# A selective scan laid out by states: sixteen states of eight channels in a tile's rows

## The chip, the cores and the metric

The kernel runs on one core of one Trainium2 chip. The metric is the device time of one execution in microseconds; three executions took 6134.04, 6134.65 and 6145.41 us, median 6134.65.

The core's engines work side by side, each through its own list of instructions in order: PE (matrix products; PEld is its loading of weights), DVE (element-wise work, reductions, the scan instruction), ACT (functions with scale and bias), POOL (element-wise work too) and SP, which here only issues transfers (DMA). They meet at semaphores.

## The reference, cut to what matters

The input is 4 images of 128 channels and 64 x 64 pixels, that is 4 x 4096 positions. Layer 0 normalizes, does a 3 x 3 depthwise convolution with a small network behind it, and then a selective scan ("Mamba"); layer 1 is attention with 4 heads over the 4096 positions of an image, and then a mixture of 8 experts of which each position takes 2. The change is in the scan. The 128 channels are cut into 4 chunks of 32, and each chunk is a sequence of its own that is widened to 64 channels `d` with 16 states `n` each:

```python
x_dbl = xin @ x_proj_w.T
dt, Bm, Cm = jnp.split(x_dbl, [R, R + N], axis=-1)
delta = jax.nn.softplus(dt @ dt_proj_w.T + dt_proj_b)
A = -jnp.exp(A_log)
dA = jnp.exp(delta[..., None] * A)                          # position, d, n
dBu = delta[..., None] * Bm[:, :, None, :] * xin[..., None]

def step(h, inp):
    dA_t, dBu_t, C_t = inp
    h = dA_t * h + dBu_t
    y = jnp.einsum('bdn,bn->bd', h, C_t)
    return (h, y)
...
y = jnp.transpose(ys, (1, 0, 2)) + D_skip * xin
out = y * jax.nn.silu(z) @ out_proj_w.T
```

So `delta` and `xin` depend on the channel and not on the state, `B` and `C` on the state and not on the channel, and `A` on both. All is float32.

## The kernel before, in words

**Units of the scan.** An image's 4096 positions are cut into 8 blocks of 512 (`BLK`). A block's 4 chunks are taken in two halves `p` of two chunks: 2 x 64 channels are the 128 rows of a tile. The scan of one block and half is 16 units, one for each state `n`; four images, eight blocks, two halves and 16 states make 1024 units (line 1110). A unit is:

- `fetched` (line 724): one transfer spreads the rows B and C of state n, which lie in DRAM as `bcd`, over the 128 rows (tile `rows`, 4 buffers, 512 KB),
- `decayed` (734): ACT makes `da` = exp(delta x A_n); A_n is a column of `amat`, one number a row,
- `scan` (739): DVE makes `h` = B x `du` (`du` is delta x xin), runs the scan instruction over the 512 positions in place, with the last column of the block before as its start (`states`), and makes `hc` = C x `h`.

The 16 `hc` of a half are to be added up into `y`. PE does this by products with the identity that accumulate in a PSUM tile (`ps_y`). In image 0 each `hc` goes through PE; in images 1 to 3 POOL first adds each odd `hc` to the even one before it, and PE takes the sum (lines 1153 to 1160). Then `scanned` (752) adds the skip term and gates.

**Where a unit's operands come from.** `inputs(b, i, p)` (675) makes `xin`, the gate `zs`, B and C (`bc`, written out to `bcd`), and on ACT and POOL `delta` by way of `e`, `ln` and `lost`, and `du`; these two stay in SBUF. `first_norm` (570) and `conv` (605) stand before it, `closed` (761) after the scan of a block: it projects, normalizes, and writes the attention's operands to DRAM.

**The order.** Nothing is planned at run time. The function runs one Python loop (line 1113) over slots and records each engine's instructions in the order in which they are called; the helper in line 445 adds a dependency from each instruction to the one before on its engine, so all instructions carry that line, and groups in the profile are told apart by their tiles. In each slot the loop

1. issues the transfers that earlier stages left (`flush`, 464), and the `rows` of the unit three slots ahead; if that unit's `inputs` are not done yet, `until` (1074) pushes the lanes on until they are,
2. lets one group of attention for an image whose scan is over run its scores: four products `sc` and two exponentials `pT` on ACT; its products with the values, `av` (two 64-column halves side by side), come at the end of the following slot (`weighted`, 910),
3. does the sum products that are due (1130): one slot after the unit in image 0, two slots after the odd unit in images 1 to 3; a PE instruction behind them waits with them,
4. has ACT save the state of the unit before (a copy of the last column, not in an image's last block) and make `da` of the next unit, and DVE do the three instructions of this unit,
5. between these, moves two lanes of generators on by half a stage each: lane Y (`group_norm`, `first_norm`, `conv`, `inputs`) and lane X (`closed`, the division and output stages of attention, the experts). Each lane has one PSUM tile, `ps_X` or `ps_Y`.

So image 0's scan has no attention beside it, images 1 to 3 have that of the image before, and the last image's attention runs alone. All transfers of the loop are in SP's list, in the order of the calls. Lane Y's temporaries rotate through four buffers (`tmp`, 488).

Of the kernel before, what the change touches and what calls it, by code (L numbers as in the profile page):

```python
# [9 lines left out]
F32 = mybir.dt.float32  # L10
# [7 lines left out]
P = 128  # L18
C = 128
EPS = 1e-5  # L20
BLK = 512
NT = BLK // P
IMG = 64
DI = 64
# [12 lines left out]
def conv_mamba_attn_moe_kernel(ctx: ExitStack, tc: tile.TileContext, t: dict):  # L37
# [35 lines left out]
    inz, cb, dtb, dsk, wbc = (load(k) for k in ("inz", "cb", "dtb", "dsk", "wbc"))  # L73
# [21 lines left out]
    amat = const.tile([P, NST], F32, name="amat")  # L95
# [579 lines left out]
    def inputs(b, i, p):  # L675

        xn, pairs = xn_of[b, i], pairs_of[b, i]
        r = slice(DI * p, DI * p + DI)
        ps = work("Y")
        summed(ps, [(inxc[:, j, :], pairs[:, p, 2 * j : 2 * j + BLK]) for j in range(2)])  # L680
        pz = work("X")
        mm(pz, inz[r, :], xn[r, 3 : 3 + BLK])
        yield
        xin = mix.tile([P, BLK], F32, name="xin", bufs=2)
        scalar.activation(xin, ps, AF.Silu, bias=cb)
        zs = mix.tile([P, BLK], F32, name="zs", bufs=4)
        scalar.activation(zs, pz, AF.Silu)
        yield

        pb = work("X")  # L690
        mm(pb[0:DI, :], wbc, xin)
        ps = work("Y")
        mm(ps, wdt, xin)
        yield
        bc = mix.tile([DI, BLK], F32, name="bc")
        scalar.copy(bc, pb[0:DI, :])
        bcd = dram.tile([2, NST, 2 * BLK], F32, name="bcd", bufs=4)
        send(bcd.rearrange("c n (k q) -> (c n k) q", k=2), bc)

        e = mix.tile([P, BLK], F32, name="e")  # L700
        scalar.activation(e, ps, AF.Abs, bias=dtb)
        scalar.activation(e, e, AF.Exp, scale=-1.0)
        ln = mix.tile([P, BLK], F32, name="ln")
        scalar.activation(ln, e, AF.Ln, bias=1.0)
        delta = mix.tile([P, BLK], F32, name="delta", bufs=2)
        scalar.activation(delta, ps, AF.Relu, bias=dtb)
        yield
        yield

        lost = mix.tile([P, BLK], F32, name="lost")  # L710
        gpsimd.tensor_scalar(lost, e, 1.0, -1.0, ALU.add, ALU.add)
        gpsimd.tensor_sub(lost, e, lost)
        gpsimd.tensor_add(ln, ln, lost)
        gpsimd.tensor_add(delta, delta, ln)
        du = mix.tile([P, BLK], F32, name="du", bufs=2)
        gpsimd.tensor_mul(du, delta, xin)
        in_of[b, i, p] = xin, zs, delta, du, bcd
        yield
        yield
        yield  # L720
# [3 lines left out]
    def fetched(b, i, p, n):  # L724

        bcd = in_of[b, i, p][4]
        w = mix.tile([P, 2, BLK], F32, name="rows", bufs=4)
        sync.dma_start(
            out=w.rearrange("p k q -> p (k q)"),
            in_=bcd[:, n, :][None].to_broadcast([DI, 2, 2 * BLK]),  # L730
        )
        return w

    def decayed(b, i, p, n):
        da = mix.tile([P, BLK], F32, name="da", bufs=3)
        scalar.activation(da, in_of[b, i, p][2], AF.Exp, scale=amat[:, n : n + 1])
        return da

    def scan(b, i, p, n, w, da):

        du = in_of[b, i, p][3]
        h = mix.tile([P, BLK], F32, name="h", bufs=3)
        vector.tensor_mul(h, w[:, 0, :], du)
        vector.tensor_tensor_scan(
            out=h, data0=da, data1=h, initial=0.0 if i == 0 else states[b % 2][:, p, n : n + 1],
            op0=ALU.mult, op1=ALU.add,
        )
        hc = mix.tile([P, BLK], F32, name="hc", bufs=5)
        vector.tensor_mul(hc, w[:, 1, :], h)
        return h, hc  # L750

    def scanned(b, i, p, y):
        xin, zs, delta, du, bcd = in_of.pop((b, i, p))
        vector.scalar_tensor_tensor(xin, xin, dsk, y, ALU.mult, ALU.add)
        gpsimd.tensor_mul(zs, xin, zs)
        gated[b, i, p] = zs
# [355 lines left out]
    even, y_of, waiting, groups, image, slot = None, {}, None, None, 0, 0  # L1112
    while slot < len(units) or due or waiting or groups or image < B or lanes["X"] or running:
# [16 lines left out]
        while due and due[0][0] <= slot:  # L1130
            _, unit, term, first = due.popleft()
            b, i, p, n = unit
            if first:
                y_of[b, i, p] = ps_y.tile([P, BLK], F32, name="y")
            mm(y_of[b, i, p], ident, term, first, n == NST - 1)
            if n == NST - 1:
# [9 lines left out]
        for ahead in range(slot if slot == 0 else slot + 1, min(slot + 2, len(units))):  # L1146
            decays[ahead] = decayed(*units[ahead])
        if slot < len(units):
            unit = units[slot]
            h, hc = scan(*unit, rows.pop(slot), decays.pop(slot))  # L1150
            old = unit, h
            b, i, p, n = unit

            if b == 0:
                due.append((slot + 1, unit, hc, n == 0))
            elif n % 2 == 0:
                even = hc
            else:
                gpsimd.tensor_add(even, even, hc)
                due.append((slot + 2, unit, even, n == 1))  # L1160
# [34 lines left out]
def _laid_out(i):  # L1195
# [11 lines left out]

    def twice(a):
        return np.repeat(a, 2, axis=0)
# [4 lines left out]
    wbc = np.zeros((P, 2, NST, 2), np.float32)  # L1214
    xdt, dtT = np.zeros((4, P), np.float32), np.zeros((4, P), np.float32)
    for c in range(2):
        d = slice(c, P, 2)
# [14 lines left out]
    for h in range(NH):  # L1232
# [19 lines left out]
        "wbc": wbc.reshape(P, -1), "alog": twice(c0["A_log"]),  # L1252
# [28 lines left out]
```

## Time and profile before

| | |
|---|---|
| median of 3 executions | 6134.65 us |
| the profiled execution | 6135.26 us; span from first to last instruction 6133.5 us |
| PE busy | 5188.5 us (85%) |
| DVE busy | 4197.3 us (68%) |
| ACT busy | 3952.4 us (64%) |
| POOL busy | 1925.1 us (31%) |
| granted PE clock, mean | 0.921 |
| transfers | 928.55 MB, 44.7% of the time of 16 engines on SP's queue |
| `pT` on ACT | 2048 x 1024 ns |
| scan on DVE, with a state | 896 x 1451 ns |
| `hc` and `h` on DVE | 1024 x 782 ns and 1024 x 777 ns |
| `hc`+`hc` on POOL | 384 x 1451 ns |
| sum products on PE | 640, two passes each, 804.2 us busy |
| `rows` from DRAM | 1024 x 512 KB, 4.2 us from issue to landing |

Times are in microseconds from the first instruction unless marked ns. A group's line gives line, engine, operation, output and inputs by tile names, the operand shapes and count, then busy time and mean duration, then the idle time of the engine just before these instructions and what ended it. The row of slices gives, for 40 equal parts of the span, an engine's busy share in tenths, and the clock that PE was granted in tenths of full speed. The chain of waits goes back from the last instruction to what released it, step by step; its shares say which work set the end. Matrix products are pipelined and their ends modelled, so that the distance between their starts is the better measure of what one costs.

### The profile page before, as it was taken

Reading aid. Unit: us, or ns where it says so; the run is one execution under the profiler, and the core shown is the slowest. Engines: PE = TensorE matmul, PEld = TensorE weight load, DVE = VectorE, ACT = ScalarE, POOL = GpSimd, SP = SyncE. Lnnn points to the kernel's source line nnn. Section 1 sums busy time; section 2 is a strip of 40 time slices with the busy share of each in tenths; the row PEclk is TensorE's granted clock in tenths of the full one; section 3 lists DMA queues with packets and bytes.
Section 4 is the critical chain, followed back from the end, with each engine's and each line's share of the span. In section 5 each row is a group of like instructions: output and inputs, shape, how many; then the busy total and the mean of one; then the engine's idle time right before and its main releaser. Section 6 shows DMA issues by size and latency. Waiting matters only on the chain.

```text
span 6133.5 us, 60705 instructions
## 1 busy us (share of the span) xinstructions
PE 5188.5 (85%) x18378; PEld 2135.6 (35%) x18378; DVE 4197.3 (68%) x7155; ACT 3952.4 (64%) x6052; POOL 1925.1 (31%) x1757
## 2 busy tenths in 40 slices
PE   4666665698899989889999898999888898999996
PEld 2222222233333333333333333333333333333332
DVE  4888887788888877778888777888777772021112
ACT  3445544577777767677777676777777765655652
POOL 2334323444344334333444344344333320000000
PEclk7777777799999999999999999999999999999996
DMA  3444554555455535555555554555554542212210
GB/s 99 163 174 164 187 178 152 171 190 170 168 184 178 188 134 181 167 170 179 187 178 181 178 168 168 177 167 174 174 167 165 170 158 79 79 64 72 74 66 13
DMA packets 359137, 928.55 MB, mean 151 GB/s; under 512 B 37633, under 2 KB 120978, under 8 KB 358802
## 3 DMA queue, kind: packets, MB, share of 16 engines
q1 hardware_dynamic: 357634, 923.80, 44.7%
q8 instruction: 148, 2.42, 0.2%
q14 instruction: 187, 1.53, 0.1%
q10 hardware_dynamic: 1168, 0.80, 0.0%
HBM read 806.95 MB, written 100.66 MB: 148 GB/s over the span
## 4 chain that ended last, share of the span: by engine, by line
PE 43%; DVE 33%; ACT 12%; POOL 5%; issue 5%; DMA 2%; SPq 0%; DVEq 0%; ACTq 0%; POOLq 0%
PE av L445 18%; DVE h L445 15%; PE ps_X L445 10%; PE sc L445 9%; DVE hc L445 5%; DVE acc L445 5%; PE y L445 4%; ACT pT L445 3%; PE ps_Y L445 3%; DVE cm L445 3%; ACT L445 2%; ACT xt L445 2%; POOL rsX L445 2%; POOL rsY L445 1%; ACT da L445 1%
## 5 line engine op out<-in xcount | busy, mean ns | idle before, releaser
L445 ACT ACTIVATE pT<-sc 128x1024 f32<-128x1024 f32 x2048 | 1986.7, 1024 | 881.2 <-PE sc L445 876.3
L445 PE MATMUL av<-pT,v 128*64 128x512 f32 x8192 | 2027.1, 616 | 0.0
L445 DVE TENSOR_TENSOR_SCAN h<-da,state,h 128x512 f32<-128x512 f32 x896 | 1299.8, 1451 | 244.0 <-ACT da L445 157.8
L445 PE MATMUL sc<-qs,ks 128*128 128x512 f32 x4096 | 1335.2, 444 | 124.5 <-ACT pT L445 77.4
L445 POOL TENSOR_TENSOR hc<-hc 128x512 f32<-128x512 f32 x384 | 557.1, 1451 | 1707.3 <-DVE hc L445 1542.9
L445 PEld LDWEIGHTS sc<-qs,ks 128*128 128x128 f32 x4096 | 714.3, 192 | 726.5 <-ACT pT L445 367.8
L445 PE MATMUL y<-hc,ident 128*128 128x512 f32 x1280 | 804.2, 718 | 181.7 <-DVE hc L445 172.5
L445 PEld LDWEIGHTS av<-pT,v 128*64 128x64 f32 x8192 | 506.9, 139 | 1168.0 <-issue 1140.3
L445 DVE TENSOR_TENSOR hc<-rows,h 128x512 f32<-128x512 f32 x1024 | 801.2, 782 | 70.9 <-DVE h L445 1.4
L445 DVE TENSOR_TENSOR h<-rows,du 128x512 f32<-128x512 f32 x1024 | 795.9, 777 | 32.3 <-POOL du L445 29.2
L445 ACT ACTIVATE da<-delta,amat 128x512 f32<-128x512 f32 x1024 | 750.2, 734 | 25.8 <-DVE h L445 24.3
L445 DVE SCALAR_TENSOR_TENSOR acc<-ps_X,pr,acc 128x128 f32<-128x128 f32 x1024 | 358.4, 350 | 304.6 <-PE ps_X L445 276.8
L445 ACT ACT_TABLE_LOAD x318 | 408.0, 1283 | 101.8 <-PE sc L445 92.1
L445 POOL TENSOR_SCALAR rsX<-mvX 128x4 f32<-128x4 f32 x97 | 52.4, 540 | 1224.3 <-DVE mvX L445 1222.7
L445 PE MATMUL ps_X<-w_ew,xf 128*128 128x512 f32 x512 | 304.3, 678 | 126.0 <-DVE acc L445 123.9
L445 PEld LDWEIGHTS y<-hc,ident 128*128 128x128 f32 x1280 | 260.3, 222 | 419.8 <-DVE hc L445 302.8
L445 DVE RECIPROCAL rden<-ps_X 128x8 f32<-128x8 f32 x64 | 13.1, 205 | 566.9 <-PE ps_X L445 566.9
L445 ACT COPY state<-h 128x1 f32<-128x1 f32 x896 | 176.3, 197 | 269.6 <-DVE h L445 269.2
L445 ACT ACTIVATE xt<-ps_Y,shiftY,rsY 128x128 f32<-128x128 f32 x380 | 142.9, 460 | 174.3 <-POOL shiftY L445 158.2
L445 DVE TENSOR_TENSOR_SCAN h<-da,h 128x512 f32<-128x512 f32 x128 | 176.9, 1382 | 57.0 <-ACT da L445 45.8
L445 POOL TENSOR_SCALAR rsY<-mvY 128x4 f32<-128x4 f32 x95 | 43.5, 458 | 532.7 <-DVE mvY L445 528.0
L445 PE MATMUL ps_Y<-ident,xt 128*128 128x128 f32 x380 | 74.7, 329 | 159.8 <-ACT xt L445 159.5
(197 smaller groups left out, 4766.6 us busy)
## 6 DMA issues: line engine op xcount, KB each, us to landing
rows<-bcd SPq DMA_DIRECT2D x1024, 512.0 KB, 4.2
ks<-kd SPq DMA_DIRECT2D x256, 512.0 KB, 5.6
v<-vd SPq DMA_DIRECT2D x256, 256.0 KB, 5.9
qs<-qd SPq DMA_DIRECT2D x64, 512.0 KB, 5.8
pairs<-xn SPq DMA_DIRECT2D x128, 128.5 KB, 2.4
qd<-hi SPq DMA_DIRECT2D x32, 512.0 KB, 6.8
qd<-lo SPq DMA_DIRECT2D x32, 512.0 KB, 5.9
vd<-vst SPq DMA_DIRECT2D x32, 512.0 KB, 7.4
```

What stands on the lines that cost most here:

```text
L445: return lambda *args, **kw: queued(op(*args, **kw))
```

## The change

Rows of a unit are now 16 states of 8 channels (row = 8 x state + channel), in place of 128 channels of one state. A block's half still has 16 units `k`, each with 8 of the 128 rows of (chunk, channel).

- B and C of a chunk, spread over the 8 channels of each state, are fetched once for 8 units (tile `bcs`, 2 buffers, 512 KB) and stay.
- `delta` and `du` are made in one tile `dd`, written to DRAM (`ddd`, 512 KB), and for each unit 8 of their rows are fetched, spread over the 16 states (`rows`, 512 KB as before). `inputs` has two more half stages for it. `da` is made from the fetched `rows`, not from the resident `delta`; `amat` has 8 columns, one for each group of 8 channels.
- `y` of a unit is a sum over its 16 states, so over rows. Four units' `hc` are kept and summed together, one slot after the fourth: for each a product with 128 x 32 weights `sel` that puts its 8 channels at 8 of 32 output rows; the four go to the four 32-row strips of the `y` tile, side by side. Sixteen products a half fill the tile, in four groups. POOL adds nothing.
- Weights, biases and `A` are laid out so that the channels stand in the order this gives (`place`).
- Buffers: `da` 3 to 2, `hc` 5 to 6, `e` and `ln` move to lane Y's four temporaries, `lost` to the place of `du`.

```diff
-        e = mix.tile([P, BLK], F32, name="e")
+        dd = mix.tile([P, 2, BLK], F32, name="dd")
+        delta, du = dd[:, 0, :], dd[:, 1, :]
+        e = tmp("Y", "e")
...
-        in_of[b, i, p] = xin, zs, delta, du, bcd
+        yield
+        yield
+        ddd = dram.tile([P, 2 * BLK], F32, name="ddd", bufs=4)
+        send(ddd, dd.rearrange("p k q -> p (k q)"))
+        in_of[b, i, p] = xin, zs, ddd, bcd
...
+    def fetched(b, i, p, k):
+        ddd, bcd = in_of[b, i, p][2:]
+        if k % 8 == 0:
+            w = mix.tile([P, 2, BLK], F32, name="bcs", bufs=2)
+            sync.dma_start(
+                out=w.rearrange("p k q -> p (k q)"),
+                in_=bcd[k // 8][:, None, :].to_broadcast([NST, P // NST, 2 * BLK]),
+            )
+            chunk[0] = w
         w = mix.tile([P, 2, BLK], F32, name="rows", bufs=4)
+        at = 32 * (k % 4) + 8 * (k // 4)
         sync.dma_start(
             out=w.rearrange("p k q -> p (k q)"),
-            in_=bcd[:, n, :][None].to_broadcast([DI, 2, 2 * BLK]),
+            in_=ddd[at : at + 8][None].to_broadcast([NST, P // NST, 2 * BLK]),
         )
-        return w
+        return w, chunk[0]
...
-        da = mix.tile([P, BLK], F32, name="da", bufs=3)
-        scalar.activation(da, in_of[b, i, p][2], AF.Exp, scale=amat[:, n : n + 1])
+        da = mix.tile([P, BLK], F32, name="da", bufs=2)
+        scalar.activation(da, w[:, 0, :], AF.Exp, scale=amat[:, k % 8 : k % 8 + 1])
...
-        vector.tensor_mul(h, w[:, 0, :], du)
+        vector.tensor_mul(h, bc[:, 0, :], w[:, 1, :])
...
-        hc = mix.tile([P, BLK], F32, name="hc", bufs=5)
-        vector.tensor_mul(hc, w[:, 1, :], h)
+        hc = mix.tile([P, BLK], F32, name="hc", bufs=6)
+        vector.tensor_mul(hc, bc[:, 1, :], h)
...
-            mm(y_of[b, i, p], ident, term, first, n == NST - 1)
-            if n == NST - 1:
+            for g, term in enumerate(four):
+                mm(y_of[b, i, p][32 * g : 32 * g + 32, :], sel[:, q, :], term, q == 0, q == 3)
+            if q == 3:
...
-            if b == 0:
-                due.append((slot + 1, unit, hc, n == 0))
-            elif n % 2 == 0:
-                even = hc
-            else:
-                gpsimd.tensor_add(even, even, hc)
-                due.append((slot + 2, unit, even, n == 1))
+            terms.append(hc)
+            if len(terms) == 4:
+                due.append((slot + 1, unit, terms))
+                terms = []
...
+    for q in range(4):
+        sel[:, :, q, q] = np.eye(8)
```

## The prediction

> **What bounds the kernel now.** First the forty slices, then the same engines by stage. The scan's units start at 101 us; image 0's end at 1078 and the last at 5026, so stage I is scan alone, stage II scan of images 1 to 3 beside attention of the image before, stage III attention alone.
>
> ```profile
> PE   4666665698899989889999898999888898999996
> DVE  4888887788888877778888777888777772021112
> PEclk7777777799999999999999999999999999999996
> ...
> 101.00:1078.00 977.00, 623.24 (x1256) 240.37 (x1257) 821.86 (x1167) 472.09 (x904) 330.44 (x296) 0.76 0.49 169
> 1078.00:5026.00 3948.00, 3513.68 (x13045) 1465.21 (x13043) 3147.66 (x5130) 2872.85 (x4441) 1549.04 (x1360) 0.96 0.52 174
> 5026.00:6133.00 1107.00, 1010.10 (x3966) 411.05 (x3964) 205.16 (x740) 584.23 (x670) 25.51 (x52) 0.95 0.19 63
> ```
>
> The stage rows give PE, PEld, DVE, ACT, POOL busy, PE clock, DMA share and GB/s. Stage I is DVE's (84%; PE 64% at a clock of 0.76). Stage II has PE at 89% and DVE at 80%; stage III is PE's. Busy shares don't say what a saved microsecond is worth, so next the chain of waits, by stage (II, then I), and a piece of II:
>
> ```profile
> by line: PE av L445 15.4%; DVE h L445 15.1%; PE ps_X L445 8.5%; PE sc L445 7.5%; DVE hc L445 5.2%; issue 5.1%; DVE acc L445 5.0%; ACT pT L445 4.7%; PE y L445 4.6%; DVE cm L445 3.7%; PE ps_Y L445 2.9%; ACT L445 2.7%; ACT xt L445 1.9%; POOL r
> ...
> by line: DVE h L445 34.0%; DVE hc L445 12.8%; PE y L445 6.7%; PE ps_X L445 5.7%; issue 4.6%; PE ps_Y L445 4.1%; ACT L445 3.9%; POOL rsY L445 3.2%; DMA rows<-bcd 2.8%; ACT xt L445 2.7%; ACT da L445 2.0%; POOL rsX L445 1.9%; DVE cm L445 1.7%;
> ...
> 3042.37 0.93 PE sc L445 x4
> 3043.30 0.86 PE y L445 x2
> 3044.16 1.87 PE av L445 x8
> ```
>
> One sum product (two passes, as each of these float32 products is) costs 0.86 us of chain; `av`, eight passes on 64 columns, costs 1.87, that is 0.47 for every two passes: those go two abreast, as their starts show:
>
> ```profile
> 3000.11 0.65 PE L445 MATMUL av<-pT,v 128*64 128x512 f32 x2
> 3000.59 0.60 PE L445 MATMUL av<-pT,v 128*64 128x512 f32 x2
> 3001.02 0.60 PE L445 MATMUL av<-pT,v 128*64 128x512 f32 x2
> ```
>
> Last the scan's own groups, stage II above stage I:
>
> ```profile
> L445 DVE TENSOR_TENSOR_SCAN h<-da,state,h 128x512 f32<-128x512 f32 x672 | 998.7, 1486 | 176.1 <-ACT da L445 111.9 <-DVE h L445 2.3 <-ACT xt L445 0.5
> L445 DVE TENSOR_TENSOR h<-rows,du 128x512 f32<-128x512 f32 x768 | 608.0, 792 | 0.0
> L445 DVE TENSOR_TENSOR hc<-rows,h 128x512 f32<-128x512 f32 x768 | 591.1, 770 | 55.9 <-DVE h L445 0.9
> L445 POOL TENSOR_TENSOR hc<-hc 128x512 f32<-128x512 f32 x383 | 555.8, 1451 | 1700.1 <-DVE hc L445 1542.9 <-PE sc L445 99.7 <-PE av L445 14.5
> L445 DVE TENSOR_TENSOR_SCAN h<-da,h 128x512 f32<-128x512 f32 x96 | 136.1, 1417 | 45.5 <-ACT da L445 36.9
> ...
> L445 DVE TENSOR_TENSOR_SCAN h<-da,state,h 128x512 f32<-128x512 f32 x224 | 301.1, 1344 | 67.9 <-ACT da L445 45.9 <-DVE h L445 0.9
> L445 DVE TENSOR_TENSOR hc<-rows,h 128x512 f32<-128x512 f32 x256 | 210.0, 820 | 14.9 <-DVE h L445 0.5
> L445 DVE TENSOR_TENSOR h<-rows,du 128x512 f32<-128x512 f32 x256 | 187.9, 734 | 32.3 <-POOL du L445 29.2 <-DMA rows<-bcd 3.0
> L445 DVE TENSOR_TENSOR_SCAN h<-da,h 128x512 f32<-128x512 f32 x32 | 40.8, 1276 | 11.5 <-ACT da L445 8.8
> ```
>
> **The change, part by part** (stage II unless said; 192 groups of four units there, 64 in stage I).
>
> 1. *Sums on PE.* 383 products cost 383 x 0.86 = 330 us. Four 32-column products abreast would cost 0.86 a group, 165 in all. Added: changes of column width. `xin`x`wbc`, 64 columns between 128-column products, takes 1.04 to 1.07 where 0.86 would do, so 0.09 a change, one or two a group: about 26. Net -139. Only 4.6% x 3948 = 182 of the 330 us stand on the chain (55%), so the gain lies between 55% (-76) and all of it, PE being 89% busy; I take three quarters: **-104**. No row shows four abreast: with two it is 330 again, one by one 660.
> [...]
>
> 2. *POOL's 383 adds go.* DVE's two multiplies and scan take 2333.9/768 = 3.04 us a unit in II and 739.8/256 = 2.89 in I, where no such adds run: 0.15 x 768 = 114 us. Their weight on the chain: `h` 15.1% x 3948 = 596 of 1743 busy (34%), `hc` alike. **-40**; ends 0 (POOL's other work stretches DVE instead) and -114.
> [...]
>
> 3. *A tighter wait.* A pair's product now waits for POOL, PE only 8 us for it in all; a group's waits for the `hc` of the slot before, one unit later, in PE's fixed order, with that slot's `av` and the lanes' products behind it. I set each start of a product against the end of that `hc`: 80 of 383 would be late, by 102 us; half the products remain: 51, and in some 40 cases the fourth product then runs alone, 0.86 each: 85 in all, 55% of it on the chain: **+45**; ends 0 and +100, as a faster PE waits more.
>
> 4. *Stage I.* The sums fall from 256 x 0.86 to 64 x 0.86; 6.7% x 977 = 65 us of them are on the chain, three quarters go: -49. But PE, idler, may lose clock: `ps_X` and `ps_Y` hold 9.8% = 96 us at 0.76; at 0.5 they cost 48 more. DVE's work stays. **-10**; ends -50 and +50.
>
> 5. *Fewer slots.* The sum of a half block is due a slot earlier, so `closed` of the last image starts at slot 1029, not 1034, and the loop written out has 1329 slots, not 1334. Stage III has 1107/310 = 3.57 us a slot, -18; four attention groups move into II (2.8 us of PE each). **-7**; ends -18 and 0.
>
> 6. *The way through DRAM.* Before the first unit the pair delta, du is now written out (512 KB; `qd<-hi`, as large, lands after 6.8 us) and fetched (4.2): **+11** at the start; ends +6 and +17. `inputs` has two more stages, so the first half block's inputs end just at the slot that fetches them (61, 93, ...). Elsewhere `du` ends 16 us before that unit's `da` starts, against 0.5 issue + 6.8 + 4.2 + 2.5 for the B/C tile fetched ahead of it = 14: hidden by the units still running; in stage I 10.4 us, and `h` 6 later. At the last block of images 0 to 2, where the loop already stops to push the lane (19.7, 31.8, 30.6 us between two units' starts against 3 to 5), 8 pushes take the place of 6, 7 and 7; at some 4 us each 16, part of it lane work done sooner, and in image 0 `du` ends 5.5 us before `h`, so some 8.5 late: **+22**; ends +9 and +40.
>
> At nothing: 512 KB a unit is fetched as before, and 192 more transfers of 512 KB (100 MB on 928) take the DMA share from 0.52 to about 0.57; cover gone, rows come late. `da` now waits for its rows: in II it starts 8.6 us or more after their issue in 99 of 100, against 4.2 (longest 9.8), and rows are freed a scan and a multiply earlier. On SP the new write waits for `du`, and rows, `ks`, `v` wait behind it; they are issued three slots (15 us) ahead. `da` with two buffers: ACT's state copy, just before it, waits for that same scan already. `e` and `ln` in the lane's four buffers, host layouts, the 64 KB `sel`: beside the start's other loads.
>
> Sum: -104 - 40 + 45 - 10 - 7 + 11 + 22 = -83. The profiled execution took 6135.3 (span 6133.5), the median is 6134.65, so they agree: 6135 - 83 = **6052**, say 6050.
>
> **Rivals.** *Two abreast only:* `av` proves two, nothing proves four. Term 1 becomes +20 for width changes, stage I gains half: 6052 + 124 + 5 = 6180, slower; it decides once a group takes over about 1.45 us. One by one: 330 x 0.75 more still, 6430. *The DRAM way shows:* if write plus fetch exceed 16 us, DVE waits at each of 28 half-block borders; 5 us each is +140, 6190. Against it: 14 by medians; for it: both run amid 170 GB/s. *Fuller relief:* PE's saving counts whole (-139), DVE's 114, no new wait, stage I -50: 5860 to 5920; for it speaks that the two engines that lead stage II's chain are relieved at once, against it the 80 late products. *Nothing moves* (the chain merely changes engine, as ACT's 73% could let it): 6120 to 6147.
>
> **How the numbers follow.** What this kernel's runs can tell from no change is about 0.2%, 12 us. Main case 0.60 (own range 5960 to 6115), two abreast 0.13, one by one 0.03, DRAM 0.10, fuller relief 0.14. Faster: 0.14 and nearly all of the main case, less 0.01 from elsewhere, 0.69; same 0.04; slower 0.27. The range 5900 to 6190 leaves out one by one and about half of DRAM and of fuller relief: some 0.16.
>
> **What would show it.** Right: `y` passes starting in fours some 10 ns apart, two rounds a group, its busy time in II near 200 us; no `hc<-hc`; scan near 1340 ns in II; PE waiting for `hc` by tens of us, not hundreds; stage II near 3870. Wrong: `y` in four or more rounds, ACT `da` waiting for `rows`, SP long on `du`, DVE idle at each border, or a clock in stage I far under 0.7 with DVE waiting for `ps_Y`.

## The result: slower by 2.3%, and the profile after

The changed kernel takes 6282.7 us, the median of 4 executions (6268.2 to 6285.9), against 6139.5 for the kernel before in the same comparison (4 executions, 6134.0 to 6145.4). The ratio is 1.0228, with a 95% interval of 1.0208 to 1.0249. The prediction, 6050 with a range from 5900 to 6190, is wrong in sign and in size. The profiled execution took 6268.2 us, with a span of 6266.2, the shortest of the four, so the views below understate the loss by some 15 us.

First the forty slices of the changed kernel, then its stages: scan alone, scan beside attention, attention alone. The columns of the stage rows are those of the rows before.

```profile
PE   4455544488888888888988889888998998999996
DVE  4777777767777777777777767777777872121122
PEclk7666666599999999999999989999999999999996
...
109.00:1186.00 1077.00, 536.37 (x1253) 170.38 (x1254) 826.99 (x1169) 475.45 (x902) 323.45 (x295) 0.62 0.70 178
1186.00:5170.00 3984.00, 3465.03 (x13832) 1372.37 (x13832) 2997.27 (x5153) 2868.83 (x4445) 997.82 (x977) 0.94 0.70 191
5170.00:6266.00 1096.00, 1001.51 (x3948) 407.30 (x3944) 199.27 (x717) 580.12 (x666) 24.23 (x51) 0.95 0.20 63
```

| | before | after |
|---|---|---|
| first unit of the scan starts at | 101 us | 109 us |
| stage I | 977 | 1077 |
| stage II | 3948 | 3984 |
| stage III | 1107 | 1096 |
| DMA share in I and II | 0.49, 0.52 | 0.70, 0.70 |

Stage I lost 100 us and stage II 36. In stage II the engines did what the change was expected to give: PE is busy 49 us less, DVE 150 less, POOL 551 less. The time is longer although the work is less, so the engines wait more. What rose is the DMA share, from about one half to 0.70, where 0.57 was predicted.

Did the summing itself do as foretold? These are the changed kernel's groups in stage II:

```profile
L445 DVE TENSOR_TENSOR_SCAN h<-da,state,h 128x512 f32<-128x512 f32 x672 | 948.4, 1411 | 274.7 <-ACT da L445 214.8 <-DVE h L445 1.9
L445 DVE TENSOR_TENSOR hc<-bcs,h 128x512 f32<-128x512 f32 x768 | 593.8, 773 | 34.1 <-DVE h L445 0.9
L445 DVE TENSOR_TENSOR h<-bcs,rows 128x512 f32<-128x512 f32 x768 | 559.9, 729 | 1.6 <-DMA rows<-ddd 1.6
L445 PE MATMUL y<-hc,w_sel 128*32 128x512 f32 x1528 | 253.0, 688 | 8.4 <-DVE hc L445 8.4
```

and, of one group of four products, the tile's own view and the timeline around it:

```profile
L445 PE MATMUL y<-hc,w_sel x8: 592/605/617, 3006.2 to 3006.6; 128*32 128x512 f32 x8
...
3006.16 1.06 PE L445 MATMUL y<-hc,w_sel 128*32 128x512 f32 x8
3007.15 1.94 PE L445 MATMUL av<-pT,v 128*64 128x512 f32 x8
```

The eight passes of a group start within 0.47 us, and 0.99 us after the first one PE is at the next products. In the trace's records four of them start 7 ns apart, and the other four 0.45 us later: they do go four abreast. `y` keeps PE busy for 253 us in stage II, against 426 before, and waits 8.4 us there for an `hc`. The scan instruction fell from 1486 to 1411 ns. That half of the change works.

The other half is the transfers. Their rows (packets, MB and the share of 16 engines' time for the queue; for each transfer its count, its size and the median from issue to landing), and the waits of SP's list:

```profile
q1 hardware_dynamic: 385426, 1024.54, 60.2%
...
rows<-ddd SPq DMA_DIRECT2D x1024, 512.0 KB, 5.8
ks<-kd SPq DMA_DIRECT2D x256, 512.0 KB, 6.1
bcs<-bcd SPq DMA_DIRECT2D x128, 512.0 KB, 6.9
...
ddd<-dd SPq DMA_DIRECT2D x64, 512.0 KB, 3.1
...
gn<-in_x SPq DMA_DIRECT2D x32, 256.0 KB, 8.2
```

```profile
SPq L445 <- DVE h L445: 1880.5, 654, 9.8
SPq L445 <- ACT bc L445: 515.8, 64, 13.3
SPq L445 <- POOL dd L445: 513.4, 64, 11.9
```

Three things are to be seen. The bytes rose by 11% (924 to 1024.5 MB), but their time rose by 38%: 60.2% of 16 x 6266.2 us is 58.9 us of engine time a MB, where 44.7% of 16 x 6133.5 was 47.5. `rows`, of the same 512 KB, land after 5.8 us instead of 4.2, and in the records of the first 250 us of scan a 4 KB packet takes 268 ns in the mean instead of 186 (the records name no tile; most of these packets are `rows`). And SP's list, on which every load of the loop stands, waits 513 us for POOL's `dd`, a wait that was not there before. ACT's `da` waits 100.5 us for `rows` in stage I alone, and DVE's `h` another 48.1.

The chain of waits, by stage (I, then II), holds these waits for transfers beside the old work:

```profile
by line: DVE h L445 17.3%; PE ps_Y L445 7.9%; DMA rows<-ddd 7.6%; POOL dd L445 6.2%; PE ps_X L445 6.2%; issue 6.2%; DMA gn<-in_x 6.1%; DVE hc L445 5.7%; POOL rsY L445 5.1%; ACT L445 3.7%; PE y L445 3.2%; ACT xt L445 2.6%; ACT da L445 2.3%; 
...
by line: PE av L445 15.2%; DVE h L445 11.1%; PE ps_X L445 8.5%; PE sc L445 7.8%; ACT pT L445 6.5%; issue 5.7%; DVE acc L445 4.6%; PE y L445 4.1%; DVE hc L445 3.8%; ACT L445 3.5%; PE ps_Y L445 3.2%; DMA gn<-in_x 3.0%; ACT xt L445 2.4%; DVE c
```

`gn` is the load of lane Y's next block. With its 6.1% of stage I and 3.0% of stage II it holds 184 us of the chain, where it was 25 before, and `rows` hold 149.

### The profile page after: what moved, and what is told of

Its sections match the earlier page's. It is cut to its first block, busy times and chain, and to the rows that moved or that the text cites. A ratio compares the mean times of both kernels' runs of the same rounds, so it can differ in the third digit from the quotient of the medians.

```text
span 6266.2 us, 62729 instructions
## 1 busy us (share of the span) xinstructions
PE 5047.0 (81%) x19146; PEld 1969.6 (31%) x19146; DVE 4046.2 (65%) x7155; ACT 3949.5 (63%) x6052; POOL 1365.6 (22%) x1373
## 3 DMA queue, kind: packets, MB, share of 16 engines
q1 hardware_dynamic: 385426, 1024.54, 60.2%
## 4 chain that ended last, share of the span: by engine, by line
PE 42%; DVE 23%; ACT 15%; DMA 7%; POOL 6%; issue 5%; SPq 1%; DVEq 0%; ACTq 0%; POOLq 0%
PE av L445 17%; DVE h L445 10%; PE ps_X L445 10%; PE sc L445 9%; ACT pT L445 4%; DVE acc L445 4%; PE ps_Y L445 4%; DVE hc L445 3%; PE y L445 3%; DMA gn<-in_x 3%; ACT L445 3%; DMA rows<-ddd 2%; ACT xt L445 2%; POOL rsY L445 2%; DVE cm L445 2%
## 5 line engine op out<-in xcount | busy, mean ns | idle before, releaser
L445 PE MATMUL av<-pT,v 128*64 128x512 f32 x8192 | 2050.0, 622 | 1.3 <-ACT avs L445 1.3
L445 DVE TENSOR_TENSOR_SCAN h<-da,state,h 128x512 f32<-128x512 f32 x896 | 1253.2, 1399 | 362.0 <-ACT da L445 280.5
L445 ACT ACTIVATE da<-rows,amat 128x512 f32<-128x512 f32 x1024 | 753.0, 736 | 150.6 <-DMA rows<-ddd 116.9
L445 DVE TENSOR_TENSOR hc<-bcs,h 128x512 f32<-128x512 f32 x1024 | 795.2, 777 | 50.4 <-DVE h L445 1.4
L445 DVE TENSOR_TENSOR h<-bcs,rows 128x512 f32<-128x512 f32 x1024 | 756.4, 739 | 49.7 <-DMA rows<-ddd 49.7
L445 PE MATMUL y<-hc,w_sel 128*32 128x512 f32 x2048 | 447.9, 738 | 140.9 <-DVE hc L445 140.9
L445 POOL TENSOR_TENSOR zs<-xin,zs 128x512 f32<-128x512 f32 x64 | 104.9, 1639 | 1280.6 <-DVE xin L445 1246.1
L445 POOL TENSOR_SCALAR dd<-e 128x512 f32<-128x512 f32 x64 | 127.0, 1985 | 826.7 <-ACT e L445 742.8
L445 DVE TENSOR_TENSOR_SCAN h<-da,h 128x512 f32<-128x512 f32 x128 | 170.1, 1329 | 63.7 <-ACT da L445 52.7
```

What stands on the lines that cost most here:

```text
L445: return lambda *args, **kw: queued(op(*args, **kw))
```

## The experiments

Two things were open: how much of the loss is in the sums (the prediction's terms 1 to 5) and how much in the transfers, and which property of the transfers costs. The first four runs separate the packets' speed, the volume and the sums; the next four the order of the work, with one more on the volume; the last four the place of the new write and what is left.

**Two rows, dealt out 64-fold.** Both spread transfers take the shape of the transfer before. The rows then hold two channels' `delta` and `du` in place of eight, and two states' B and C in place of sixteen; bytes and counts are the same.

```diff
-            in_=ddd[at : at + 8][None].to_broadcast([NST, P // NST, 2 * BLK]),
+            in_=ddd[at : at + 2][None].to_broadcast([DI, 2, 2 * BLK]),
...
-                in_=bcd[k // 8][:, None, :].to_broadcast([NST, P // NST, 2 * BLK]),
+                in_=bcd[k // 8][0:2][None].to_broadcast([DI, 2, 2 * BLK]),
```

> The changed kernel, but each transfer of `rows` and of `bcs` reads only two rows of DRAM, 64 times each in the outermost dimension (the shape that `rows` had before), in place of 8 rows 16 times and 16 rows 8 times in a 16-fold outermost dimension; the same 512 KB in the same number of packets, other values (so the scan's operands are not the reference's). Theory A (the shape of the two new transfers makes their 4 KB packets slow: some 283 ns in the first 250 us of the scan against 182 ns before, so that `da` and `h` wait for rows): landing of `rows` falls from 5.8 to about 4.2 us, ACT's 117 us of waiting for rows nearly go, the time falls by 100 us or more, to 6180 or less. Theory B (the added bytes and the way out to DRAM and back cost it): no change, 6270 to 6290. Theory C (PE at a lower clock, or waiting for `hc`, costs it): no change either, 6260 to 6290.

Measured: 6198.8 us (1.0106, interval 1.0089 to 1.0123). That is 84 us less than the changed kernel; theory A has the direction and the landing, but had asked for 100 or more.

```profile
q1 hardware_dynamic: 385426, 1024.54, 48.7%
...
rows<-ddd SPq DMA_DIRECT2D x1024, 512.0 KB, 4.2
bcs<-bcd SPq DMA_DIRECT2D x128, 512.0 KB, 5.2
```

The same bytes now cost 48.7% of 16 x 6193.1 us, 47.1 us a MB, and `rows` land after 4.2 again. So it was not volume that slowed the packets, but how these two transfers are laid out. On the chain of waits `rows` falls from 149 to 31 us and `gn` from 184 to 65: the slow packets cost time in these two loads above all, though SP still waits 511 us for `dd`. The 84 us are about a third of the 251 us that will be found missing below.

**One row, in the 16 x 8 shape.** Only `rows` differ: all 128 rows hold one channel's `delta` and `du`, read from a single row of DRAM.

```diff
-            in_=ddd[at : at + 8][None].to_broadcast([NST, P // NST, 2 * BLK]),
+            in_=ddd[at : at + 1][None].to_broadcast([NST, P // NST, 2 * BLK]),
```

> The changed kernel, but each transfer of `rows` reads one row of DRAM 128 times, in the 16 x 8 shape of the changed kernel (so delta and du of one channel stand for eight; the values are not the reference's). If the slow packets come from how the 16-fold outermost dimension is dealt out to the engines and to the tile's rows, nothing moves: rows land after 5.8 us, 6270 to 6290. If they come from reading 8 different rows of DRAM, packets are as fast as before, and the time is that of the run with two rows (6180 or less).

Measured: 6292.3 us (1.0259, 1.0238 to 1.0279); 4 KB packets of 253 ns in the same stretch, where the changed kernel's take 268, and `rows` land after 6.1 us. Reading fewer rows of DRAM does not help. With the run before, this points to the shape: 16 outermost pieces of 8 neighbouring rows are slow (253 and 268 ns a packet), 64 pieces of two are fast (188). Why the one shape is slower is not shown, as the records hold no addresses, and that a single row is slow for a reason of its own is not excluded.

**B and C fetched once.** 126 of the 128 `bcs` transfers are left out, and all blocks use the first one's B and C.

```diff
-        if k % 8 == 0:
+        if k % 8 == 0 and (b, i, p) == (0, 0, 0):
```

> The changed kernel without the transfers of `bcs` after the first two: 126 of 128 x 512 KB are left out, and every unit uses the B and C of the first half block (values not the reference's). Theory A: a twelfth of the slow transfers go, those that stand just ahead of a `rows`; 6230 to 6270. Theory B (added bytes): two thirds of the 100 MB that came on top go, so at least half of the loss: 6210 or less. Theory C: 6270 to 6290.

Measured: 6211.7 us (1.0127, 1.0107 to 1.0148), just outside theory B's range and below theory A's: with slow packets 66 MB cost 71 us. The 4 KB packets stay at 259 ns, so these bytes are not what makes them slow.

**The sums alone.** The kernel before with the four side-by-side products and without POOL's adds, `hc` 6 and `da` 2 buffers. Each product takes 32 columns of the identity, so that only a quarter of each `hc` enters `y` and the rest of the sum is left out; the products and their waits are those of the change.

```diff
-            mm(y_of[b, i, p], ident, term, first, n == NST - 1)
-            if n == NST - 1:
+            for g, term in enumerate(four):
+                mm(
+                    y_of[b, i, p][32 * g : 32 * g + 32, :], ident[:, 32 * g : 32 * g + 32], term,
+                    q == 0, q == 3,
+                )
+            if q == 3:
```

> The kernel before with the change's sums alone: four units' `hc` kept, four products with 32 columns of the identity side by side one slot after the fourth, nothing added on POOL, `hc` six and `da` two buffers (y then holds sums over channels' quarters that are not the reference's); transfers, `delta`, `du` and `rows` as before. By the prediction's terms 1 to 5 it takes 6139 - 104 - 40 + 45 - 10 - 7 = 6023 us. If the sums or the lower clock of PE cost the time (theory C), it is at or above the kernel before, 6140 to 6280.

Measured: 6031.6 us (0.9833, 0.9817 to 0.9849), 103 us less than before. By stage, in the columns of the stage rows above:

```profile
101.00:1117.00 1016.00, 562.85 (x1257) 169.06 (x1258) 830.59 (x1168) 473.67 (x904) 317.64 (x295) 0.65 0.48 163
1117.00:4916.00 3799.00, 3363.31 (x13737) 1348.37 (x13736) 2954.79 (x5129) 2856.68 (x4429) 995.11 (x977) 0.96 0.54 181
```

Stage II gives 149 us and stage I loses 39, while its clock falls from 0.76 to 0.65 with fewer products on PE. The sums are a gain, and the changed kernel stands 6282.7 - 6031.6 = 251 us above them. All of that belongs to the way of delta, `du`, B and C through transfers, and to the order that came with it; the prediction gave it 33 us.

Slow packets explain 84. The next four runs ask for the other 167.

**Two empty half stages.** The sums alone, and in `inputs` the two half stages that the change adds ahead of its write, with nothing in them.

```diff
+        yield
+        yield
         in_of[b, i, p] = xin, zs, delta, du, bcd
```

> The kernel before with the four side-by-side products (6031.6 us when they were alone) and, added to it, the changed kernel's two half stages in the inputs, with nothing in them: no transfer, no spread of delta, B and C fetched as before. With them the loop written out has 1329 slots, as the changed kernel's, against 1335. Theory 'order': of the 251 us that the changed kernel loses against the sums alone, 84 are the slow packets, and most of the remaining 167 comes from the two half stages, through which the inputs of a half block are due just when they are fetched and the lanes are pushed in lumps: 6130 to 6190, stage II at 3890 or more. Theory 'transfers': the order costs little and the 167 are the added transfers and what waits for them: 6015 to 6050, stage II near 3800.

Measured: 6168.2 us (1.0056, 1.0039 to 1.0072): two steps that do nothing cost 137 us.

```profile
101.00:1135.00 1034.00, 536.29 (x1258) 171.04 (x1258) 828.46 (x1168) 472.88 (x904) 324.89 (x296) 0.63 0.49 160
1135.00:5068.00 3933.00, 3436.94 (x13832) 1366.46 (x13832) 2993.10 (x5154) 2870.51 (x4445) 996.72 (x977) 0.95 0.53 175
5068.00:6165.00 1097.00, 1001.45 (x3946) 406.79 (x3942) 198.97 (x716) 580.16 (x666) 24.23 (x51) 0.95 0.20 63
```

Against the sums alone stage I is 18 us longer, stage II 134, and only 14 come back in stage III. No transfer changed, and the DMA share is 0.53. What changed is when lane Y does what. The loop fetches the rows of a unit three slots ahead, and stops to push both lanes until that unit's `inputs` are done. From the order written out: with the sums alone it stops at 10 of the 31 borders between blocks, with 25 pushes; with the two half stages at 29, with 50. The units then go more unevenly: of the 767 distances from one unit's start to the next in stage II, 232 are 6 us or more instead of 180. A block of image 1 takes 165 us instead of 153. By images the scan takes 18, 96 and 46 us more and, in the last, 8 less, where the loop stops at 5, 7, 5 and 2 borders more than with the sums alone. On the chain of stage II it is PE's work that grew: `y` from 98 to 161 us, `av` from 580 to 642, `sc` from 288 to 331. Whether the pushes themselves do this, or that every later step of lane Y now falls beside another unit, was not taken apart.

**Two rows, B and C once.** The first run, with only the first half block's `bcs`: volume with fast packets.

```diff
-        if k % 8 == 0:
+        if k % 8 == 0 and (b, i, p) == (0, 0, 0):
...
+            in_=ddd[at : at + 2][None].to_broadcast([DI, 2, 2 * BLK]),
```

> The changed kernel with two DRAM rows spread over 64 in every transfer of rows (wrong channels, as in the run with two rows: 6198.8) and with the B/C tile fetched for the first half block only and kept for all others (126 transfers of 512 KB, 66 MB, left out; the values of the other blocks are left out). Theory 'volume': what the two-row run still loses against the sums alone (167 us) is in good part the added 66 MB, as leaving them out gained 71 us with slow packets: 6110 to 6140. Theory 'order' or 'waits at SP': with fast packets the volume costs little: 6175 to 6200.

Measured: 6177.1 us (1.0068, 1.0051 to 1.0085): 22 us less than the 6198.8 with all of them, in the range of theory 'order'. The volume that cost 71 us in the 16 x 8 shape costs 22 in the 64 x 2 shape.

**Two rows, no added half stages.** The first run without the two half stages; `ddd` is sent right after `du` is written down.

```diff
         gpsimd.tensor_mul(du, delta, xin)
-        yield
-        yield
         ddd = dram.tile([P, 2 * BLK], F32, name="ddd", bufs=4)
```

> The changed kernel with two DRAM rows spread over 64 in the transfers of rows and of B and C (wrong values, 6198.8 us) and without the two half stages: delta and du are sent to DRAM right after the call that makes them, 1335 slots. Theory 'order': it loses only the added volume against the sums alone: 6040 to 6090. Theory 'waits at SP': the write now waits longer for POOL's du at the head of SP's list, and rows wait behind it: 6200 to 6260, SP waiting for dd above the 513 us of the changed kernel. Theory 'volume': 6180 to 6200, no change.

Measured: 6128.5 us (0.9991, 0.9981 to 1.0000; ten executions, 6116.6 to 6136.9). It is 70 us less than with the half stages, half of what they cost the sums alone. But this edit does two things: the write, which stood two half stages behind `du` in the changed kernel, now comes right after it. None of the three ranges holds it, as two theories seem right in part: the order gives back time, and SP's wait for `dd` grew, from 511 to 609 us. What such a wait does, in image 0, in the timelines of SP and of DVE:

```profile
240.53 0.51 SPq L445 DMA_DIRECT2D bcd<-bc  x1
241.13 0.55 SPq L445 DMA_DIRECT2D rows<-ddd  x1
256.59 0.33 SPq L445 DMA_DIRECT2D ddd<-dd  x1
257.01 0.51 SPq L445 DMA_DIRECT2D rows<-ddd  x1
257.57 0.66 SPq L445 DMA_DIRECT2D bcs<-bcd  x1
258.40 0.51 SPq L445 DMA_DIRECT2D rows<-ddd  x1
258.96 0.59 SPq L445 DMA_DIRECT2D gn<-in_x  x1
```

```profile
259.22 0.69 DVE L445 TENSOR_TENSOR hc<-bcs,h 128x512 f32<-128x512 f32 x1
265.61 0.55 DVE L445 TENSOR_SCALAR gn<-gn,gm,gr 128x512 f32<-128x512 f32 x1 [5.70 <-DMA gn<-in_x]
266.07 0.68 DVE L445 TENSOR_TENSOR h<-bcs,rows 128x512 f32<-128x512 f32 x1
```

SP issues nothing for 15 us: its next entry is the write, and POOL's last multiply into `dd` ends at 256.56. Behind the write stand three more spread transfers, and then the load of lane Y's next block (`gn`). DVE's list has that block's first step between two units, and stands still for 5.7 us, and the unit behind it with it. In blocks 1 to 7 of image 0 the unit after this step starts 7.1 to 9.4 us after the one before it, where it is 3.1 to 3.9 with the sums alone.

**No added half stages, B and C early.** The changed kernel, every transfer in its own shape: `inputs` without the two half stages, and a B/C tile fetched four units ahead of its first use (the first of a block excepted).

```diff
-        if k % 8 == 0:
+        if k % 8 == 4 and (k, p) != (12, 1):
+            after = (b, i, p, 1) if k == 4 else (b, i, 1, 0)
+        else:
+            after = (b, i, p, 0) if (k, p) == (0, 0) else None
+        if after:
```

> The changed kernel with all values as they were, without the two half stages, and with the B/C tile fetched four units ahead of its first use (the first of a half block excepted), so that it no longer stands right before the rows of the same unit. Packets stay slow. Theory 'order': about 110 to 150 below the changed kernel's 6282.7: 6130 to 6175. Theory 'volume': 6260 to 6290. Theory 'waits at SP': 6280 to 6340.

Measured: 6173.9 us (1.0070, 1.0053 to 1.0087), 109 less than the changed kernel, within theory 'order'. What the early fetch of B and C gives by itself was not tried. It stands 45 above the two-row run without half stages, where slow packets cost 84 with them; since the two also differ in when B and C are fetched, the 45 is not the price of the packets alone.

**The write after `du`.** The run before, with the send in the place of the second of the empty half stages at the end of `inputs`.

```diff
-        ddd = dram.tile([P, 2 * BLK], F32, name="ddd", bufs=4)
-        send(ddd, dd.rearrange("p k q -> p (k q)"))
-        in_of[b, i, p] = xin, zs, ddd, bcd
         yield
         yield
+        ddd = dram.tile([P, 2 * BLK], F32, name="ddd", bufs=4)
+        send(ddd, dd.rearrange("p k q -> p (k q)"))
+        in_of[b, i, p] = xin, zs, ddd, bcd
         yield
```

> The run without the two half stages and with the B/C tile fetched early (6173.9 us, all values as they were), with the write of delta and du moved two half stages later inside `inputs`: it takes the place of the second of the three empty half stages that the kernel before had at the end, so the number of half stages and the slots (1335) stay those of the kernel before. Theory 'waits at SP': the write stood at the head of SP's list until POOL had made du, and the rows of unit 6 of a block and group_norm's loads behind it came late (unit 6 starts 8.1 us after unit 5 in image 0 and 9.1 in image 3, against 3.3 and 7.1 with the sums alone); now it finds du done: 6085 to 6125, SP waiting for dd under 150 us. Theory 'landing': the rows of a half block's first units wait for the write to land, whenever it is issued, and it is now issued nearer to them: 6165 to 6200.

Measured: 6109.5 us (0.9967, 0.9956 to 0.9979), 64 less. The time is as theory 'waits at SP' gave it, but its sign is not: SP still waits 453 us for `dd`, not under 150. It waits as often (64 times). What shrank is what waits behind it: the chain of waits holds 13 us of `gn`'s load in stage II, where it was 86.

**The same with fast packets.** The two-row run without half stages, with the write moved in the same way.

```diff
-        ddd = dram.tile([P, 2 * BLK], F32, name="ddd", bufs=4)
-        send(ddd, dd.rearrange("p k q -> p (k q)"))
-        in_of[b, i, p] = xin, zs, ddd, bcd
         yield
         yield
+        ddd = dram.tile([P, 2 * BLK], F32, name="ddd", bufs=4)
+        send(ddd, dd.rearrange("p k q -> p (k q)"))
+        in_of[b, i, p] = xin, zs, ddd, bcd
```

> The changed kernel with the write of delta and du placed as in the run before this one, no added half stages, and two DRAM rows spread over 64 in the transfers of rows and of B and C (wrong values; the same without the moved write took 6128.5 us). Theory 'waits at SP': with schedule, packets and SP's wait all undone, only the volume is left against the sums alone (6031.6): 6040 to 6070. Theory 'landing' or 'volume': 6110 to 6140.

Measured: 6084.7 us (0.9919, 0.9902 to 0.9936), 44 less than with the early write. It missed 6040 to 6070 by 15: more is left than the volume. The write stands two half stages behind `du` here, as in the changed kernel, so this run against the two-row run with the added half stages (6198.8) gives the price of those alone: 114 us.

**The write issued by POOL.** As the run with B and C early, with one line changed.

```diff
-        send(ddd, dd.rearrange("p k q -> p (k q)"))
+        gpsimd.dma_start(out=ddd, in_=dd.rearrange("p k q -> p (k q)"))
```

> As the run without the two half stages and with the B/C tile fetched early (6173.9 us, all values as they were), but the write of delta and du is issued by POOL, which makes du just before, in place of SP, with no other move. Theory 'waits at SP': nothing of SP's list waits for du any more, and the write starts as early as it can: 6080 to 6120, unless POOL's own issue of a transfer costs it more than 2 us each (64 of them). Theory 'landing': the same time as before it, 6165 to 6180.

Measured: 6102.5 us (0.9957, 0.9940 to 0.9974), 71 less than from SP. SP's list in the same stretch:

```profile
240.57 0.49 SPq L445 DMA_DIRECT2D bcd<-bc  x1
241.17 7.33 SPq L445 DMA_DIRECT2D rows<-ddd  x3
248.55 0.58 SPq L445 DMA_DIRECT2D gn<-in_x  x1
251.80 0.52 SPq L445 DMA_DIRECT2D rows<-ddd  x1
```

The load of `gn` goes out 10 us earlier, the 15 us hole is gone, and the unit that waited starts 3.1 us after the one before it. On the chain of the whole scan `gn` holds 8 us, where it held 141. The transfers themselves take as long as before: the two queues together hold 60.3 + 1.7% of the time of 16 engines, against 61.4% on one. Moving 64 of more than 2000 issues was worth 71 us: what went is not the time to issue them (0.33 us for one in the timeline of the two-row run above, so by estimate 21 us for 64) but a wait of 609 us for `dd` at the head of a list in order; 146 us of waiting for the write's landing (11 before) came in its place.

This is the fastest version here that leaves out and replaces nothing. It beats both kernels: 180 us below the changed kernel, and 0.43% below the one before.

**The rest.** The run with fast packets and the write moved, and with `bcs` fetched once.

```diff
-        if k % 8 == 0:
+        if k % 8 == 0 and (b, i, p) == (0, 0, 0):
```

> The run with two rows spread over 64, no added half stages and the write placed after du (6084.7 us, wrong values), with the B/C tile fetched for the first half block only (126 transfers of 512 KB left out; the values of the other blocks are left out). It stands 53 us above the sums alone (6031.6), with some 7 of it at the start. Theory 'volume': these 66 MB are most of the rest: 6040 to 6055. Theory 'landing': the rest is the way of delta and du through DRAM itself (rows of a half block's first unit wait for du, the write and the fetch one after the other), and stays: 6070 to 6090.

Measured: 6066.9 us (0.9886, 0.9869 to 0.9902): between the two expectations. The volume is worth 18 us, and 35 stay.

Put in a row, first up from the sums alone, adding parts of the change, then down from the changed kernel:

| step | us | time after it |
|---|---|---|
| the sums alone | | 6031.6 |
| two empty half stages in `inputs` | +137 | 6168.2 |
| delta, `du`, B and C by way of DRAM, in fast packets | +31 | 6198.8 |
| shape of the spread transfers | +84 | 6282.7 |

| step taken back | us | time after it |
|---|---|---|
| the changed kernel | | 6282.7 |
| shape of the spread transfers | -84 | 6198.8 |
| two half stages, the write still two half stages behind `du` | -114 | 6084.7 |
| 66 MB of B and C | -18 | 6066.9 |
| what is left: delta and `du` go through DRAM at all | -35 | 6031.6 |

The 31 us of the first table hold all else that the change does: 100 MB more, the new write and its wait in SP's list, the later start (108.5 us against 101.0), other buffers. So in the changed kernel's own order the wait for `dd` can hardly cost more than 31 us in the 64 x 2 shape; in the 16 x 8 shape it was not priced apart. The 44 to 71 us that the place and the issuer of the write were worth were measured where it comes right after `du`, which the changed kernel does not do.

About 8 of the last 35 are the later start (108.7 us against 101.0). The rest was not taken apart; that `dd` is one buffer, where delta and `du` had two each, was not tried either. Nor do the steps have prices of their own: the half stages cost 114 or 137, the volume 18, 22 or 71, according to what else was there.

## Why the prediction was wrong

**The sums, terms 1 to 5: right in sum.** They gave -104 - 40 + 45 - 10 - 7 = -116; the run with the sums alone gave -103. The parts were off against each other.

- *Term 1, sums on PE:* four abreast holds. On the chain of stage II `y` falls from 182 to 98 us with the sums alone, where 104 was taken off. In the changed kernel, with the half stages, it is back at 163.
- *Term 2, POOL's adds:* the three DVE instructions of a unit fall from 3.04 to (948.4 + 130.0 + 593.8 + 559.9)/768 = 2.91 us in stage II, 102 us where the sum allowed 114, 130.0 being the scans without a state; with the sums alone they fall to 2.86, 137 us. The forecast of 1340 ns for the scan was too low: 1387 with the sums alone, 1411 after.
- *Term 3, a tighter wait:* 85 us of late products were counted, and PE waited 18 for `hc` with the sums alone and 8 after. Probably a group that starts late has its `hc` soon, since PE was itself behind. With this term near nothing the stage II of the forecast is the measured one: -149 against -144 without it.
- *Term 4, stage I:* near the upper end. The clock fell from 0.76 to 0.65 with the sums alone (0.62 after), and stage I lost 39 us, where -10 was taken and +50 was that end. On its chain `y` falls from 66 to 30 us and `ps_Y` rises from 40 to 69, as that end supposed, but `ps_X` does not rise, and a net 45 us of other work came on, ACT's above all; so the clock is shown for a part only.
- *Term 5, fewer slots:* the 1329 slots are right but their cause is not. The sums alone need 1335; the half stages bring 1329, by pushes, and the 14 us that they save at the end are bought with ten times that before it (152).

**Term 6 is the step that failed,** with what stood under "at nothing". Against its +33 stand 251 us: 84 for the shape of the transfers, which it put at nothing, 114 to 137 for the two half stages, which it priced at three borders only, and the rest for the way through DRAM itself.

- *"512 KB a unit is fetched as before."* The bytes are, the shape is not. A 4 KB packet took 268 ns instead of 186: 84 us with all else as in the change. The price of the new transfer was taken from the row of the old one, which has the same size and another layout. The DMA share was put at 0.57 by counting bytes; it is 0.70.
- *"`inputs` has two more stages, so the first half block's inputs end just at the slot that fetches them (61, 93, ...)."* This was seen and only asked whether the write would land in time. That the loop now stops at nearly each border to push was costed at the three borders where it had already stopped. There the distances are 23.1, 32.5 and 39.0 us, 12.5 more in all where 22 was taken; the cost of the half stages lies elsewhere, in images 1 and 2 above all: 137 us on the sums alone, 114 from the changed kernel with fast packets. By which step of the order it comes about stays open.
- *"On SP the new write waits for `du`, and rows, `ks`, `v` wait behind it; they are issued three slots (15 us) ahead."* What was counted behind the write were the scan's and attention's loads, and not lane Y's own `gn`, which has no such lead; DVE waits for it between two units. `gn` holds 184 us of the changed kernel's chain, but 65 with fast packets and the same wait at SP, so here it is late through the packets more than through the write. What the write adds was measured only where it comes right after `du` (44 to 71 us).
- *The +33 itself:* with fast packets and the half stages' own cost taken out, the way through DRAM costs 31. That this is so near is partly luck: the start is 8 us later for +11, the write lands in 3.1 us and not 6.8, and waits at SP and of `da` that stood at nothing are in it.

**The rivals.** "The DRAM way shows" came nearest, with 6190, and its sign, SP long on `du`, was seen. But it priced 5 us at 28 borders from one cause, write plus fetch over 16 us; the largest part came from the order of the work and the next from the packets' shape, neither of which it names. "Two abreast" and "one by one" are excluded by the starts 7 ns apart. Of "fuller relief" the sums alone show a part: no new wait to speak of, but 149 us in stage II, not PE's 139 and DVE's 114 together, and a loss in stage I.

**The signs.** Passes in fours, two rounds a group and no `hc<-hc` came as given, `y` at 253 rather than near 200 us, the scan at 1411 rather than near 1340 ns, stage II at 3984 rather than near 3870. Of the signs for wrong, two came in full: ACT `da` waiting for `rows`, 117 us in all, and SP long on `dd`, 513 us. Two came in part: DVE's `h` waits 50 us for `rows`, 11 times and not at each border, and the clock in stage I is 0.62.

## What to carry to other kernels

Two transfers of the same 512 KB had different prices here because of their shape, 5.8 and 4.2 us to landing and 84 us in all: before a row of the profile is used for a new one, compare how the two deal their pieces out, not only the bytes. In a list that is executed in order, a new wait can cost through whatever stands behind it with the least lead, as `gn` did in the runs with the early write (DVE stood still 5.7 us for it in the timeline shown), so go through every entry behind it, those of other lanes too, or give the wait to the engine that makes the data. And where the order of work is written out by a loop with deadlines, a step that does nothing can still move the work around it, for 137 us here; try it empty and alone before blaming what it carries.

## What the runs showed that was not expected

- Four products of 128 x 32 run fully abreast: their first passes start 7 ns apart. In stage II, at a mean granted clock of 0.94, the second ones come 0.45 us later in 127 of the 164 groups whose records show this start, and 0.86 us later in most of the others. In stage I, at 0.62, 36 of 64 groups start so, and in 24 of them the two rounds are 0.86 us apart.
- Same queue, same 512 KB, same 128 packets of 4 KB: 186 ns a packet in 64 pieces of two rows and 268 in 16 pieces of eight (188 when put back), 47 against 59 us of engine time a MB.
- PE's granted clock in stage I falls from 0.76 to 0.65 when its busy time falls from 623 to 563 us in a span that is 4% longer, and `ps_Y` on the chain rises from 40 to 69 us there, which takes back part of what fewer products gave.
- The scan instruction is slower in the changed kernel than with the sums alone (1411 against 1387 ns in stage II), though POOL does the same work in both (998 and 995 us busy there); what does that was not tried.
